# The order of a fused attention and FP4 feed-forward block: a table of places instead of a formula of due dates

## The chip, the cores and the metric

The kernel runs on one core of a Trainium2 chip. Its engines work side by side, each through its own queue of instructions in the order in which the program lists them: TensorE (PE, matmuls; PEld is its loading of weights), VectorE (DVE), ScalarE (ACT), GpSimd (POOL) and SyncE (SP, which here only issues transfers; ACT issues a few as well). The metric is the time of one execution on the device in microseconds (us), the median of several runs.

## What is computed

The input has 16 sequences of 512 rows of 256 numbers, in float32. The reference, cut to what matters:

```python
q, k = favor(x @ Wq + bq), favor(x @ Wk + bk)  # 16 heads of 16 numbers
# favor(a): exp(a - max) over a head's 16 numbers, divided by (their sum + 1e-6)
v = x @ Wv + bv
context = ((q @ k.T) / (q.sum(-1) + 1e-6)) @ v  # no softmax: linear in k.T @ v
x = layernorm(x + context @ Wo + bo)
# fp4(a): in blocks of 16, scale = max|a| / 6, each number rounded to the FP4 grid, times scale
gate, up = fp4(x) @ fp4(w_gate).T, fp4(x) @ fp4(w_up).T  # 704 wide
h = silu(gate) * up
x = layernorm(x + fp4(h) @ fp4(w_down).T)
```

## The kernel before, in words

A tile has 128 rows; a sequence (a batch `b`) has four tiles, worked on as two pairs, so there are 32 pairs `i`. Each stage is a function that hands its operations to a `Plan`:

- `project` (per pair): TensorE turns x (L636), ScalarE copies it to SBUF (`transposed`, L639, tile xT), four groups of two matmuls give q and k of a tile (L778), VectorE adds the bias (L781) and takes each head's maximum (L786), GpSimd subtracts it (L790).
- `features` (per batch): ScalarE's exp (L801), VectorE's sums and reciprocals (L803 to L814), GpSimd's scaling (L820).
- `key_values` (per batch): a sum over k on VectorE (L829, ks), k times x on TensorE (L836), copied by ScalarE (L843), times the weights of v (L852, L853), masked by VectorE (L857, kvT), times Wo (L864), copied by ScalarE (L870, M).
- `attend` (per pair): q turned (L636, copied at L639 as qT), times M (L892), then `norm`: sum with the input on VectorE (L733), mean and variance on ScalarE (L740, L742), the root on GpSimd (L746 to L748), applied on ScalarE (L755). The result goes to DRAM (L903) and is read back later (L910).
- `weight_scales` and `fp4_exact`: the three weights of the feed-forward part are quantised once, on VectorE, ScalarE and GpSimd (L515 to L534 and L563 to L584), in 12 pieces, and turned by TensorE (L597, L620).
- `quantise` (per pair): `codes` finds scales and FP4 codes of x on VectorE and ScalarE (L655 to L668); VectorE transposes them in blocks (L921, L691); four kinds of transfers through DRAM regroup the codes (L676, L681) and spread the scales over the partitions (L699, L704); GpSimd multiplies both (L929, xqT).
- `gate_up` (per pair): 16 matmul operations of 352 columns (L957; the chip runs each as two matmuls), silu on ScalarE (L962), product on VectorE (L964), `codes` of h, transposes (L1002), the same kinds of transfers, and GpSimd's product (L1009, hq, in four quarters). The last pair takes a shorter way, by L977 on VectorE and transposes on TensorE (L991).
- `down` (per pair): 12 matmul operations for each of its two tiles u (L1026), `norm`, and the output (L1038). The last two pairs have another norm (L718 to L725).

What sets the order is the plan. Every operation has an engine, a cost in us that the source estimates (`t_pe`, `t_dve`, `t_act`, `t_ts`, `t_pool` and figures beside the operations) and a **due date**, a multiple of `PAIR` = 25 that a formula gives from batch, pair and stage (`due_at`, `wdue`). `Plan.order` runs a list schedule of these estimates while the kernel is built: for each engine it finds the operations whose inputs are planned, and the earliest start of each, from its inputs' ends plus `LAG` where they are on another engine, the engine's own free time, free buffers and PSUM banks, and a port that `port=True` operations of VectorE share with GpSimd. Among those that can start within 0.02 us of the earliest on that engine it takes the one with the lowest due date:

```python
first = min(t for t, _ in c)
t, o = min(((t, o) for t, o in c if t <= first + 0.02), key=lambda x: (x[1].due, x[1].at))
if best is None or t < best[0]:
    best = t, o
```

The sequence that results is written out as the program. On the chip each engine follows its part of it and waits for data where it must; the planned times are not used there. `dma` makes two operations of a transfer: its issue on a queue (SP or ACT) and its flight.

Of the kernel before, what the change touches and what calls it, by code (L numbers as in the profile page):

```python
# [17 lines left out]
P = 128  # L18
# [8 lines left out]

LAG = 0.3

PAIR = 25.0  # L30
# [13 lines left out]
MAGIC_U = 1.5 * 2.0**29  # L44
UNTIE = 1.0 + 2.0**-17


# [44 lines left out]
class Op:  # L92
    __slots__ = ("eng", "us", "fn", "due", "preds", "succs", "left", "bufs", "new", "start", "end", "table", "port", "name", "at")


class Plan:
# [47 lines left out]
    def order(self):  # L144
# [32 lines left out]
        def start(o, at):  # L177
            if o.port:
                at = max(at, port)
            for p in o.preds:  # L180
                at = max(at, p.end + (LAG if p.eng != o.eng else 0.0))
            taken = {}
            shared = [b for b in o.new if isinstance(b, Bank) and id(b) not in ends]
            if shared:
                found = find(shared[0].args[0], [b.tag for b in shared])
                if found is None:
                    return None
                at = max(at, found[0])
            for b in o.new:
                if id(b) in ends or isinstance(b, Bank):  # L190
                    continue
                key = id(b.args[0]), b.tag
                ring, n = rings.setdefault(key, []), taken.get(key, 0)
                taken[key] = n + 1
                if len(ring) + n >= b.bufs:
                    left, end = ends[id(ring[n - b.bufs])]
                    if left:
                        return None
                    at = max(at, end + LAG)
            return at  # L200

        while len(out) < len(self.ops):
# [16 lines left out]
            o.start, o.end = t, t + us  # L219
            free[o.eng] = o.end  # L220
            if o.port:
# [11 lines left out]
            for b in o.bufs:  # L233
                left, end = ends.get(id(b), (b.users, 0.0))
                ends[id(b)] = left - 1, max(end, o.end)
            for s in o.succs:
# [9 lines left out]
def t_pe(n):  # L246
    return 2 * (n / 1200.0 + 0.002)


def t_dve(n):  # L250
    return 0.15 + n / 960.0


def t_act(n):
    return 0.16 + n / 1200.0

# [5 lines left out]
def t_pool(n):  # L262
    return 0.07 + n / 525.0


@with_exitstack
def tile_favor_fp4_block(
# [229 lines left out]
    def weight_scales(src, src_b, n, at, name, due):  # L497
# [37 lines left out]

        op("DVE", 11 * fast + 0.0063 * nb, due, rest, ins=[pb], outs=[sc_b, *iv])
        return part, sc_b, iv

    def fp4_exact(src, src_b, scales, sc_b, iv, k, name, due):
# [7 lines left out]
        def b3(ap):  # L547
# [5 lines left out]
        pw, px = (psum("pg", f"{t}_{name}{k}") for t in ("pw", "px"))  # L553
        d, g, a = t_dve(F2), t_pool(F2), t_act(F2)
        tt, gt, act = nc.vector.tensor_tensor, nc.gpsimd.tensor_tensor, nc.scalar.activation
# [25 lines left out]
        op("ACT", a, due, lambda: act(y(), upper(m()), AF.Identity, bias=magic[:, 2:3], scale=UNTIE), ins=[M], outs=[px])  # L581
        op("DVE", t_ts(F2), due, lambda: nc.vector.tensor_scalar(c(), lower(y()), 6, None, ALU.logical_shift_left),
           ins=[px], outs=[pr])
# [58 lines left out]
    def codes(src, xn, sq, dst, key, n, scales, at, name, due, sat=None):  # L642
# [18 lines left out]

        op("DVE", 0.27 + 0.0073 * nb, due, scale, ins=[(amax, key)], outs=[(nscale, key), (inv, key)])
        op("DVE", t_dve(n), due, lambda: nc.vector.scalar_tensor_tensor(  # L663
# [8 lines left out]
    def regroup(src, dst, n, tag, name, due):  # L672


        d = Buf(dr, [P, 4, n], "g" + tag, 3, f"g_{name}", U32)
        dma(f"g{name}", 3.0, due, lambda: nc.sync.dma_start(d.tile, src.tile), ins=[src], outs=[d])  # L676

        def back():
            rows = d.tile.rearrange("(a i) q n -> i a q n", i=32)
            for q in range(4):  # L680
                nc.sync.dma_start(dst[32 * q : 32 * q + 32, :, :], rows[:, :, q, :])  # L681

        dma(f"h{name}", 3.5, due, back, ins=[d], outs=[dst], issue=1.8)

    def spread_scales(nscale, G, dst, tag, name, due, holds=()):
# [7 lines left out]
            nscale.tile.rearrange("p (u g r) -> p g r u", u=2, r=n),  # L693
        ), ins=[nscale], outs=[sT], port=True)
        d = Buf(dr, [2 * n, G, P], "d" + tag, 3, f"d_{name}")

        def write():
            for a in range(0, P, 32):
                nc.sync.dma_start(d[:, :, a : a + 32], sT[a : a + 32, :, :])  # L699

        dma(f"w{name}", 4.0, due, write, ins=[sT], outs=[d], issue=1.8)
        into, dst_b = dst

        dma(f"r{name}", 3.0 + 0.7 * G, due, lambda: nc.sync.dma_start(  # L704
            into(), d.tile.rearrange("(r u) g t -> r (u g t)", u=2).unsqueeze(1).to_broadcast([n, 8, 2 * G * P])),
            ins=[d], outs=[dst_b], holds=holds)

    def norm(pr, add, dst, name, due, ins, r, junk, us=range(2)):
# [3 lines left out]
        if n == 1:  # L712
# [9 lines left out]

            op("DVE", 2 * t_dve(D) + 0.1, due, stats, ins=[(pr, key)] + ins, outs=[(r, key), st, mv])
            op("POOL", 0.7, due, lambda: nc.gpsimd.tensor_tensor(rstd.tile, mv[:, 1:2], neg_half[:, :1], ALU.pow), ins=[mv], outs=[rstd])
            op("DVE", t_dve(D), due, lambda: nc.vector.tensor_scalar(  # L725
# [10 lines left out]

        op("DVE", n * (t_dve(D) + 0.06), due, total, ins=[(pr, key)] + ins, outs=[(r, key), rs])

# [10 lines left out]

        op("ACT", 0.35 + 0.6 * n, due, square, ins=[(r, key), rs], outs=[(dst, key), var, nm])  # L750
        op("POOL", 1.1, due, root, ins=[nm], outs=[var, rstd, nb])

# [5 lines left out]

        op("ACT", 0.6 * n, due, apply, ins=[(r, key), nb, rstd], outs=[(dst, key)])

# [33 lines left out]
    def features(b, due):  # L794
# [20 lines left out]

        op("DVE", 1.2, due, recip, outs=[s, r], port=True)
        for t in range(TPB):
# [6 lines left out]
    def key_values(b, due):  # L824
# [3 lines left out]
        ks = buf([D], "ks", 2, f"ks_{b}")  # L828
        op("DVE", t_dve(TPB * D), due, lambda: nc.vector.tensor_reduce(  # L829
            ks.tile, qk[:, :, D:].rearrange("p t d -> p d t"), AX.X, ALU.add), ins=[qk], outs=[ks])  # L830
# [24 lines left out]
        kvT = buf([DC, P], "kvT", 2, f"kvT_{b}")  # L855
        op("PE", DC * (DC + 1) * t_pe(P), due, mm_kv, ins=[xk, ks, wqkv_in], outs=[pkv], holds=[kvT], name="kv")
        op("DVE", t_dve(DC * P), due, lambda: nc.vector.tensor_tensor(  # L857
# [18 lines left out]
    def attend(b, p, due):  # L876
# [7 lines left out]
        xb = buf([2, D], "xb", 2, f"xb_{i}")  # L884
        op("POOL", 1.4, due, lambda: nc.gpsimd.tensor_tensor(xb.tile, x[:, two, :], twice(b_o), ALU.add),  # L885
           ins=[x, wo_in], outs=[xb])
# [15 lines left out]
        d = Buf(dr, [P, 2, D], "x1", NP, f"dx1_{i}")  # L902
        dma(f"wx1_{i}", 3.0, due, lambda: nc.scalar.dma_start(d.tile, x1.tile), ins=[x1], outs=[d], queue="ACT")  # L903
        st[i] = {"d": d}


    def quantise(i, due):
        x1 = st[i]["x1"] = buf([2, D], "x1", X1, f"x1_{i}")
        d = st[i]["d"]
        dma(f"rx1_{i}", 3.5, due - PAIR, lambda: nc.sync.dma_start(x1.tile, d.tile), ins=[d], outs=[x1])  # L910
        n = 2 * D
# [10 lines left out]
            xw.tile.rearrange("p q (u t) -> p q u t", u=2),  # L922
            xc.tile.bitcast(U32).rearrange("p (u q t) -> p q u t", u=2, q=4)), ins=[xc], outs=[xw], port=True)
        regroup(xw, xcT, 2 * 32, "x", f"x{i}", due)
# [3 lines left out]
        for u in range(2):  # L928
            op("POOL", t_pool(D), due, lambda u=u: nc.gpsimd.tensor_tensor(  # L929
                xqT[:, DC * u : DC * (u + 1), :].rearrange("p c (a t) -> p c a t", t=32),  # L930
# [6 lines left out]
    def gate_up(i, due):  # L937
# [32 lines left out]
        if i >= NP - LAST:  # L970
            for u in range(2):
# [9 lines left out]

                op("DVE", t_dve(FF), d, dequantise, ins=[(hc, u), (scales[1], u)], outs=[hd], port=True)
                for j, (gs, n) in enumerate(((range(TG - 1), P), (range(TG - 1, TG), LW))):
# [3 lines left out]
                    def tr(gs=gs, n=n, pt=pt, hd=hd):  # L987
# [6 lines left out]
                    eng, copy = (("ACT", nc.scalar.copy), ("DVE", nc.vector.tensor_copy))[j]  # L994
                    op(eng, t_act(k * P), d, lambda u=u, gs=gs, n=n, k=k, pt=pt, copy=copy: copy(
                        hq()[:n, u, gs[0] : gs[-1] + 1, :, :].rearrange("p g c t -> p (g c) t"), pt[:n, :k, :]),
# [4 lines left out]
        for u in range(2):  # L1001
            op("DVE", 0.15 + TG * P / 960.0, d, lambda u=u: nc.vector.transpose(  # L1002
                hw.tile.rearrange("p q (u g t) -> p u q g t", u=2, g=TG)[:, u], words()[:, u]),
               ins=[(hc, u)], outs=[(hw, u)], port=True)
        regroup(hw, hcT, 2 * TG * 32, "h", f"h{i}", d)
        spread_scales(scales[1], TG, (lambda: flat()[:, NQ : NQ + 2 * TG * P], (both, "s")), "h", f"h{i}", d)
        for u in range(2):
            for c in range(2):
                op("POOL", t_pool(TG * P), d, lambda u=u, c=c: nc.gpsimd.tensor_tensor(  # L1009
                    hq()[:, u, :, c, :].rearrange("p g (a t) -> p g a t", t=32),  # L1010
# [4 lines left out]
    def down(i, due):  # L1015
# [6 lines left out]
        for u in range(2):  # L1022
            for f in range(2 * TG):
# [4 lines left out]
                    start=f == 0, stop=f == 2 * TG - 1,  # L1028
                ), ins=[(both, f"{u}{c}{int(g == TG - 1)}"), wdT_b], outs=[(pd, u)], holds=[r], name="down")
        y = buf([2, D], "y" if i < NP - 1 else "yl", 1, f"y_{i}")  # L1030
        out2 = out[b, 2 * p * P : 2 * (p + 1) * P, :].rearrange("(u p) d -> p u d", p=P)

        for us in ((0,), (1,)) if i >= NP - 2 else (range(2),):
# [4 lines left out]
            dma(f"y{i}_{us[0]}", 2.5, due, lambda t=t, eng=eng: eng.dma_start(out2[:, t, :], y[:, t, :]),  # L1038
                ins=[(y, None if len(us) == 2 else us[0])], queue=q)

# [24 lines left out]
    for i in range(NP):  # L1065
        quantise(i, (i - 1.2) * PAIR)
        gate_up(i, i * PAIR)
        down(i, (i + 3) * PAIR)

    with tc.manual_schedule():  # L1070
# [47 lines left out]
```

## Time and profile before

| | us |
|---|---|
| runs | 792.51, 789.62, 791.81 |
| their median | 791.81 |
| the profiled execution, first to last instruction (span) | 792.0 |
| TensorE busy in it | 768.6 (97%) |
| VectorE busy | 656.7 (83%) |
| GpSimd busy | 455.9 (58%) |
| ScalarE busy | 416.5 (53%) |
| mean granted clock of TensorE | 0.995 |
| transfers | 89.23 MB, mean 113 GB/s |

The times are device times of whole runs; the profile is of one more execution, whose span is 0.2 us over the median. A row of the profile names the source line, the engine, the operation and what it writes and reads, then how often it ran, how long it was busy and the mean of one in ns; behind a second bar stands the idle time of the engine just before such instructions and what ended it. A row of busy times by stage gives the stretch, its length, then the busy time of each engine with the number of its instructions, the granted clock of TensorE, the share of the transfer engines in use, and GB/s.

### The profile page before, as it was taken

The page shows a single profiled execution, that of the slowest core. Times are in us where ns is not written, and L with a number is a line of the kernel's source. Part 1 is how long each engine was busy: PE and PEld are TensorE (multiplying, and loading weights), DVE is VectorE, ACT ScalarE, POOL GpSimd, SP SyncE. Part 2 cuts the span into 40 slices and gives each one's busy share as a digit, 9 for nine tenths or more (in the row PEclk, how much of TensorE's full clock was granted, in tenths as well). Part 3 has the DMA queues.
Part 4 walks back from the last instruction along what each step waited for, and adds up shares of the span by engine and source line. Part 5 has one row for each costly group of instructions (what it writes and reads, how often), then busy time and mean ns, then how long its engine had stood idle before and what let it go on. Part 6 is the DMA issues. An engine that isn't in the chain of part 4 may idle for free.

```text
span 792.0 us, 10915 instructions
## 1 busy us (share of the span) xinstructions
PE 768.6 (97%) x3118; PEld 552.5 (70%) x3118; DVE 656.7 (83%) x1340; ACT 416.5 (53%) x893; POOL 455.9 (58%) x602
## 2 busy tenths in 40 slices
PE   7999999989998999999999999999999999999996
PEld 3567657657676777767777777777777777777774
DVE  2998999999888798697697798888878988778784
ACT  2347766868887783544545444444334444344441
POOL 5668788889887755574554435434533543543633
PEclk9999999999999999999999999999999999999998
DMA  9112411211111044404335454554554554464441
GB/s 277 45 55 86 142 53 54 82 60 62 54 53 62 30 129 133 118 37 124 100 112 138 145 171 136 152 149 134 149 154 135 145 149 140 125 179 129 136 130 41
DMA packets 104348, 89.23 MB, mean 113 GB/s; under 512 B 44512, under 2 KB 87904, under 8 KB 104288
## 3 DMA queue, kind: packets, MB, share of 16 engines
q1 hardware_dynamic: 90704, 71.49, 31.8%
q10 hardware_dynamic: 13584, 17.04, 6.0%
q8 instruction: 25, 0.41, 0.2%
q14 instruction: 35, 0.29, 0.1%
HBM read 53.28 MB, written 35.21 MB: 112 GB/s over the span
## 4 chain that ended last, share of the span: by engine, by line
PE 62%; DVE 12%; DMA 8%; POOL 8%; issue 4%; ACT 4%; SPq 2%; ACTq 0%; POOLq 0%; DVEq 0%
PE bank L957 26%; PE bank L1026 14%; PE bank L778 8%; PE bank L892 5%; PE bank L836 5%; POOL hq L1009 3%; DMA out_dram<-y 3%; DVE qk L781 2%; PE bank L636 2%; DVE mx L786 2%; DMA hcT<-g_h 2%; SPq L681 1%; POOL xqT L929 1%; DVE fs L803 1%; PE bank L852 1%
## 5 line engine op out<-in xcount | busy, mean ns | idle before, releaser
L957 PE MATMUL bank<-w_guT,xqT 128*128 128x352 f32 x1024 | 311.3, 459 | 0.0
L957 PEld LDWEIGHTS bank<-w_guT,xqT 128*128 128x128 f32 x1024 | 193.8, 190 | 100.4 <-ACT g L962 0.2
L1009 POOL TENSOR_TENSOR hq<-hcT,hq 128x384 f32<-128x384 bf16 x124 | 127.3, 1058 | 179.3 <-DMA hcT<-g_h 101.4
L1026 PE MATMUL bank<-w_dT,hq 128*128 128x256 f32 (+1 forms) x768 | 173.1, 379 | 1.1 <-DVE r L718 1.1
L1026 PEld LDWEIGHTS bank<-w_dT,hq 128*128 128x128 f32 (+1 forms) x768 | 144.9, 190 | 27.5 <-issue 1.9
L778 PE MATMUL bank<-w_qkv,xT 128*128 128x512 f32 x256 | 120.8, 602 | 3.8 <-DVE qk L781 1.9
L964 DVE TENSOR_TENSOR h<-bank,g 128x352 f32<-128x352 f32 x128 | 65.7, 515 | 50.9 <-ACT g L962 24.1
L962 ACT ACTIVATE g<-bank 128x352 f32<-128x352 f32 x128 | 57.6, 458 | 87.7 <-PE bank L957 77.8
L666 ACT ACTIVATE sq<-h,magic 128x704 f32<-128x704 uint16 x64 | 56.2, 878 | 79.2 <-DVE h L663 78.6
L820 POOL TENSOR_TENSOR qk<-qk,fr 128x512 f32<-128x512 f32 x64 | 67.0, 1073 | 20.5 <-DVE fr L814 18.9
L790 POOL TENSOR_TENSOR qk<-qk,mx 128x512 f32<-128x512 f32 x64 | 67.4, 1068 | 19.2 <-DVE mx L786 19.0
L778 PEld LDWEIGHTS bank<-w_qkv,xT 128*128 128x128 f32 x256 | 46.6, 193 | 45.4 <-issue 35.8
L755 ACT ACTIVATE y<-r,nb_d,rstd_d 128x256 f32<-128x256 f32 x60 | 32.6, 591 | 59.2 <-POOL nb_d L748 59.2
L929 POOL TENSOR_TENSOR xqT<-xcT,xs 128x256 f32<-128x256 bf16 x64 | 46.3, 740 | 27.6 <-DMA d_h<-sT_h 23.4
L836 PE MATMUL bank<-qk,x 128*128 128x256 f32 x256 | 59.7, 387 | 2.1 <-ACT qT L639 2.1
L892 PE MATMUL bank<-M,qT 128*128 128x256 f32 x256 | 59.6, 381 | 1.8 <-ACT M L870 1.8
L655 DVE TENSOR_REDUCE bank<-h 128x44 f32<-128x704 f32 x64 | 57.1, 893 | 1.6
L663 DVE SCALAR_TENSOR_TENSOR h<-h,bank 128x704 f32<-128x704 f32 x64 | 56.7, 886 | 2.1
L836 PEld LDWEIGHTS bank<-qk,x 128*128 128x128 f32 x256 | 49.5, 195 | 12.7 <-ACT qT L639 3.4
L781 DVE TENSOR_TENSOR qk<-bank,b_qkv 128x512 f32<-128x512 f32 x64 | 43.0, 681 | 18.3 <-PE bank L778 17.9
L892 PEld LDWEIGHTS bank<-M,qT 128*128 128x128 f32 x256 | 47.8, 190 | 13.2 <-ACT M L870 3.8
L885 POOL TENSOR_TENSOR xb<-x,b_o 128x512 f32<-128x512 f32 x32 | 41.0, 1285 | 22.8 <-DVE r L733 22.7
(137 smaller groups left out, 1083.3 us busy)
## 6 DMA issues: line engine op xcount, KB each, us to landing
g_h<-hw SPq DMA_DIRECT2D x31, 384.0 KB, 2.8
hcT<-g_h SPq DMA_DIRECT2D x124, 96.0 KB, 2.4
hq<-d_h SPq DMA_DIRECT2D x31, 384.0 KB, 4.1
dx<-x1n ACTq DMA_DIRECT2D x32, 256.0 KB, 2.0
x<-dx SPq DMA_DIRECT2D x32, 256.0 KB, 3.1
x<-_attn_hidden_states_dram SPq DMA_DIRECT2D x15, 512.0 KB, 3.5
out_dram<-y ACTq DMA_DIRECT2D x30, 256.0 KB, 3.3
xs<-d_x SPq DMA_DIRECT2D x32, 128.0 KB, 2.5
```

The costliest lines, as they stand in the source:

```text
L655: op("DVE", t_dve(n), due, lambda: nc.vector.tensor_reduce(amax[:, g], b3(src()), AX.X, ALU.max, apply_absolute_value=True), ins=[src_b], ...
L778: op("PE", t_pe(D2), due, lambda c=c, u=u, pqk=pqk: nc.tensor.matmul(pqk.tile, xT[:, 2 * c + u, :], w_qkv[:, c, :D2], start=c == 0, stop=c ...
L781: op("DVE", t_dve(D2), due, lambda t=t, pqk=pqk: nc.vector.tensor_tensor(qk[:, t, :], pqk.tile, b_qkv[:, :D2], ALU.add), ins=[pqk], outs=[ ...
L790: op("POOL", t_pool(D2), due, lambda g=g: nc.gpsimd.tensor_tensor(qk3()[:, g, :], qk3()[:, g, :], bcast(mx[:, g], HD), ALU.subtract), ins= ...
L820: nc.gpsimd.tensor_tensor(f3, f3, bcast(r[:, t * 2 * H : (t + 1) * 2 * H], HD), ALU.mult)
L836: nc.tensor.matmul(pxk[:, c * D : (c + 1) * D], x[:, t, c * P : (c + 1) * P], qk[:, t, D:], start=t == 0, stop=t == TPB - 1,)
L892: nc.tensor.matmul(pu(pa.tile)[:, u, :], qT[:, 2 * u + c, :], M[:, c, :], start=c == 0, stop=c == DC - 1,)
L957: op("PE", t_pe(F2), due + u * 0.2 * PAIR, lambda c=c, u=u, lo=lo, ps_=ps_: nc.tensor.matmul(ps_[:, :F2], xqT[:, 2 * u + c, :], w_guT[:, c ...
L962: op("ACT", t_act(F2), due, lambda g=g, pg=pg: nc.scalar.activation(g.tile, pg[:, :F2], AF.Silu), ins=[pg], outs=[g], table="silu")
L964: op("DVE", t_dve(F2), due, lambda g=g, h=h, pu_=pu_, k=k: nc.vector.tensor_tensor(h[:, k * F2 : (k + 1) * F2], pu_[:, :F2], g.tile, ALU.m ...
L1009: op("POOL", t_pool(TG * P), d, lambda u=u, c=c: nc.gpsimd.tensor_tensor(hq()[:, u, :, c, :].rearrange("p g (a t) -> p g a t", t=32), hcT. ...
L1026: op("PE", t_pe(D), due, lambda f=f, g=g, c=c, n=n, u=u: nc.tensor.matmul(pu(pd.tile)[:, u, :], hq()[:n, u, g, c, :], w_dT[:n, f, :], star ...
```

## The change

No operation is added or taken away. Three things change in the plan, all of them used only while the kernel is built.

First, the due dates are replaced. A string holds two digits of base 91 for each of the 3939 operations in the order in which the source makes them; the number, from 0 to 1915, takes the place of `o.due`, just ahead of `order`. The table was found by a search. Some operations share a number.

Second, the estimates and lags are taken from a trace: `LAG` falls from 0.3 to 0.04; a matmul's result is there 0.165 us after its end for all but TensorE itself; a flight's end counts with 0.09 us in place of the lag; an engine is free again a little ahead of an operation's end (`OVER`). Lags now hold between operations of one engine too, but for TensorE. Many costs get new figures.

Third, three block transposes of VectorE (L691, L921, L1002) no longer share GpSimd's port in the plan, and the matmuls of `down` for tile 1 come after those for tile 0.

```diff
-LAG = 0.3
+LAG = 0.04
+DRAIN = 0.165
+OVER = {"DVE": 0.083, "ACT": 0.095, "POOL": 0.041}
+LANDED = 0.09
...
+DIGITS = "#$%&'()*+,-./0123456789:;<=>?@ABCDEFGHIJKLMNOPQRSTUVWXYZ[]^_`abcdefghijklmnopqrstuvwxyz{|}~"
+PLACES = (
+    "#3)<#5+B###%#B#$&k#2#?&B#@#9$.$1'<'C#<(v#=#:$i#>#;$}$4'R'M'l#,#(#'#&#-#.'r#c(k($')&U&}#7'('%'9+s)+&i'6(#(:#*'x'$'h&l'@'k"
...
-                at = max(at, p.end + (LAG if p.eng != o.eng else 0.0))
+                at = max(at, p.end if p.eng == o.eng == "PE" else p.done + LAG)
...
-            free[o.eng] = o.end
+            o.done = o.end + (DRAIN if o.eng == "PE" else LANDED - LAG if o.eng.startswith("DMA") else 0.0)
+            free[o.eng] = o.end - OVER.get(o.eng, 0.0)
...
-                ends[id(b)] = left - 1, max(end, o.end)
+                ends[id(b)] = left - 1, max(end, o.done)
...
 def t_pe(n):
-    return 2 * (n / 1200.0 + 0.002)
+    return 2 * (n / 1200.0 + 0.0027)
 def t_dve(n):
-    return 0.15 + n / 960.0
+    return 0.155 + n / 960.0
 def t_act(n):
-    return 0.16 + n / 1200.0
+    return 0.165 + n / 1200.0
 def t_pool(n):
-    return 0.07 + n / 525.0
+    return 0.075 + n / 520.0
+def t_mix(n):
+    return 0.19 + n / 475.0
...
-        op("DVE", 11 * fast + 0.0063 * nb, due, rest, ins=[pb], outs=[sc_b, *iv])
+        op("DVE", 2.0 + 0.015 * nb, due, rest, ins=[pb], outs=[sc_b, *iv])
...
-        dma(f"g{name}", 3.0, due, lambda: nc.sync.dma_start(d.tile, src.tile), ins=[src], outs=[d])
+        dma(f"g{name}", 2.4, due, lambda: nc.sync.dma_start(d.tile, src.tile), ins=[src], outs=[d])
...
-        dma(f"h{name}", 3.5, due, back, ins=[d], outs=[dst], issue=1.8)
+        dma(f"h{name}", 2.0, due, back, ins=[d], outs=[dst], issue=1.85)
...
-        ), ins=[nscale], outs=[sT], port=True)
+        ), ins=[nscale], outs=[sT])
...
-        dma(f"w{name}", 4.0, due, write, ins=[sT], outs=[d], issue=1.8)
+        dma(f"w{name}", 1.6, due, write, ins=[sT], outs=[d], issue=1.7 + 0.25 * G)
...
-        dma(f"r{name}", 3.0 + 0.7 * G, due, lambda: nc.sync.dma_start(
+        dma(f"r{name}", 1.3 + 0.75 * G, due, lambda: nc.sync.dma_start(
...
-        op("DVE", t_dve(TPB * D), due, lambda: nc.vector.tensor_reduce(
+        op("DVE", 1.95, due, lambda: nc.vector.tensor_reduce(
             ks.tile, qk[:, :, D:].rearrange("p t d -> p d t"), AX.X, ALU.add), ins=[qk], outs=[ks])
...
-        dma(f"rx1_{i}", 3.5, due - PAIR, lambda: nc.sync.dma_start(x1.tile, d.tile), ins=[d], outs=[x1])
+        dma(f"rx1_{i}", 2.7, due - PAIR, lambda: nc.sync.dma_start(x1.tile, d.tile), ins=[d], outs=[x1])
...
-                op("POOL", t_pool(TG * P), d, lambda u=u, c=c: nc.gpsimd.tensor_tensor(
+                op("POOL", t_mix(TG * P), d, lambda u=u, c=c: nc.gpsimd.tensor_tensor(
...
-                ), ins=[(both, f"{u}{c}{int(g == TG - 1)}"), wdT_b], outs=[(pd, u)], holds=[r], name="down")
+                ), ins=[(both, f"{u}{c}{int(g == TG - 1)}"), wdT_b] + [(pd, 0)] * u, outs=[(pd, u)], holds=[r], name="down")
...
+    assert len(PLACES) == 2 * len(plan.ops)
+    for o in plan.ops:
+        hi, lo = PLACES[2 * o.at : 2 * o.at + 2]
+        o.due = DIGITS.index(hi) * len(DIGITS) + DIGITS.index(lo)
```

L691 is shown with its `port=True` gone; L921 and L1002 lose theirs in the same way.

## The prediction

> **What bounds the kernel now.** I read the page first, then the busy times by stage, then the chain that ended last, then the instructions in order of time around the holes. The page says that TensorE is nearly full:
>
> ```profile
> span 792.0 us, 10915 instructions
> ...
> PE 768.6 (97%) x3118; PEld 552.5 (70%) x3118; DVE 656.7 (83%) x1340; ACT 416.5 (53%) x893; POOL 455.9 (58%) x602
> ```
>
> A busy PE need not be at its peak, so I take its real pace from runs of back-to-back matmuls in the chain (start, length, line, count):
>
> ```profile
> 214.43 6.01 PE bank L778 x14
> ...
> 249.49 0.44 PE bank L636 x4
> ...
> 253.84 3.45 PE bank L836 x16
> ...
> 259.88 0.45 PE bank L852 x4
> ...
> 473.11 5.18 PE bank L1026 x24
> 478.29 9.47 PE bank L957 x32
> ```
>
> Length over count gives 0.429 us (512 columns), 0.110 and 0.1125 (128), 0.2156 and 0.2158 (256) and 0.296 (352). With the counts of the groups, L957 takes 1024 x 0.296 = 303.1, L1026 768 x 0.2158 = 165.7, L778 256 x 0.4293 = 109.9, L836 and L892 256 x 0.2156 = 55.2 each, L864 64 x 0.2156 = 13.8, L636 256 x 0.110 = 28.2, L852 128 x 0.1125 = 14.4, L853 64 x 0.11 = 7.0, and the 46 transposes of L597, L620 and L991 about 5.3. The sum is **757.8 us**: the work of TensorE, which no order changes. The span holds 34.2 us more. 4.3 of it lie before the first matmul (4.26 in the timeline), 5.4 after the last one (it starts at 786.4). The other 24.5 are spacing over that pace, added up from the starts of neighbouring matmuls in the trace: 3.5 in 0 to 20, **17.3 in 20 to 260, under 0.2 in 260 to 760**, 3.7 after. The stages show the same (PE, PEld, DVE, ACT, POOL busy):
>
> ```profile
> 0.00:20.00 20.00, 15.09 (x41) 7.78 (x42) 6.11 (x7) 4.22 (x6) 10.58 (x22) 1.00 0.93 277
> 20.00:260.00 240.00, 229.40 (x1008) 161.59 (x1007) 220.91 (x394) 166.10 (x352) 193.78 (x239) 0.99 0.20 66
> 260.00:300.00 40.00, 40.00 (x166) 28.15 (x166) 33.44 (x71) 29.31 (x63) 25.70 (x35) 1.00 0.32 95
> 300.00:760.00 460.00, 460.00 (x1805) 336.60 (x1804) 377.30 (x830) 208.19 (x455) 213.62 (x292) 1.00 0.47 134
> 760.00:792.00 32.00, 24.14 (x105) 18.34 (x103) 18.90 (x42) 8.65 (x21) 12.22 (x17) 0.94 0.23 71
> ```
>
> So the kernel is bound by TensorE, but the loss is all in the first third and the last 30 us. VectorE is 92% busy in 20 to 260 and 82% in 300 to 760.
>
> The Trainium skill (Perfetto Trace Analysis, Identifying the Most-Contended Engine) would judge TensorE's headroom by its weight-load share, not its busy time. By that, 460 − 336.6 = 123 us would be free in 300 to 760, and the gain could be ten times what follows; the spacing there shows none, and the measurement decides.
>
> **What the holes are.** The largest, at 241.4, with the ACT rows ahead of it and the PE rows on both sides:
>
> ```profile
> 240.12 1.88 PE L778 MATMUL bank<-w_qkv,xT 128*128 128x512 f32 x4
> ...
> 241.02 0.49 ACT L742 ACTIVATE x1n<-r,nm_a 128x256 f32<-128x256 f32 x1
> ...
> 241.51 1.07 ACT L755 ACTIVATE x1n<-r,nb_a,rstd_a 128x256 f32<-128x256 f32 x2
> ...
> 243.44 0.59 ACT L639 COPY qT<-bank 128x512 f32<-128x512 f32 x1
> ...
> 244.08 5.41 PE L836 MATMUL bank<-qk,x 128*128 128x256 f32 x16 [2.08 <-ACT qT L639]
> ```
>
> The transposes for qT were done by 240.3, but their copy to SBUF stood on ScalarE behind two norms that nobody was waiting for. The cost is 2.2 us of idle, and then 1.7 more: the sixteen matmuls of L836 take 5.41 us here and 3.45 us at 253.84, and the granted clock is 0.57 in 245 to 249. The others have the same make: kvT (L857) waits on VectorE behind twelve instructions of one weight-scale operation (L515 to L534, 37.0 to 42.3), 1.3 us; M (L870) 0.6, 1.3 and 0.4; xT (L639) 0.5, 0.5, 0.5, 0.4 and 0.8; L781 0.5, 0.9, 0.9 and 0.5; a weight tile (L580) 1.2; L820 0.7. In each, something on VectorE, ScalarE or GpSimd that TensorE needs next stands behind something it needs later. An order can mend that.
>
> **The change part by part.** It adds and removes no instruction and no transfer, so each cost below is that of a moved place.
>
> *Estimates of the plan.* They run before the kernel is built; on the chip they cost nothing. What they alter is what the plan believes. The old plan charges L829 0.15 + 1024/960 = 1.22 us, where its row has 1.949 (x16): 11.7 us of VectorE, all in batches' chains, that it did not see. It charges L1009 0.07 + 384/525 = 0.80, where the row has 1.058 (x124): 32 us of GpSimd. The new figures are 1.95 and 1.00. For transfers it was too long: 5.1 + 0.45 us for hq<-d_h, where the median from issue to landing is 4.1; the new figure is 3.55 + 0.45. One figure stays too short: the weight scales at 37.0 take 5.3 us, old plan 4.8, new 4.6; once, 0.7 us at most.
>
> *Lag, drain, overlap, the port.* The lag between engines falls from 0.3 to 0.04 us, with 0.165 more behind a matmul. Three transposes (L691, L921, L1002) may stand beside GpSimd's work. Rows: 574 ns for L1002 where 0.15 + 384/960 gives 550; so 62 x 0.024 = 1.5 us of VectorE at most, hidden in the 82.7 us that it idles in 300 to 760.
>
> *u = 1 of down after u = 0.* TensorE runs 24 down matmuls of a pair in a row already; 0 to 0.9 us at the end, where two matmuls waited for L718.
>
> *Places.* A place decides only between operations of one engine whose earliest starts lie within 0.02 us, so the table is no timetable; data and buffers come first. All queues are reordered, SP's and ACT's DMA queues too.
>
> **The sum.** Before 10 us nothing moves: TensorE waits for loads and runs at half pace (L778 every 0.85 us), 3.1 us. The four holes from 15.7 to 42 (0.46, 0.46, 0.70, 1.26: 2.9) fall where only the first batches are loaded; I take a third, 1.0. The rest of 20 to 260 is 17.3 − 2.4 = 14.9 us. Between nothing and all of it I take four fifths, 11.9, by VectorE's row: it has 240 − 220.9 = 19.1 us idle in this stage, so with 12.9 taken out it still has 6, and what does not fit has 82.7 us later. At the end 3.7 us: half of it is the last pair's own chain (h, codes, L977, transposes), so a third, 1.2. In 260 to 760 nothing can be gained. Together 14.1: 792.0 − 14.1 = **778 us**. All 21.5 us of movable holes would give 770.5. The median of the runs shown, 791.81, is 0.2 under the span, so I leave the figure.
>
> The skill's clock rule (TensorE: Matmul & The Clock Gate, Part 1) sets half clock after an idle window of about 3.4 us. Here 2.1 us of idle was followed by it. By the rule the 1.7 us would not count with this hole, and the sum would be 779; I go by the row.
>
> **Rivals.** *The supply becomes the bound.* With no holes the steady part starts earlier, but its inputs need not. In pair 10 the last quarter of hq was written at 480.7 and L1026 began at 487.6; in pair 27 it is
>
> ```profile
> 734.56 3.87 POOL L1009 TENSOR_TENSOR hq<-hcT,hq 128x384 f32<-128x384 bf16 x4 [9.98 <-PE bank L957]
> ```
>
> written at 738.4, while L1026 begins at 736.71 and needs the last quarter only near its end. The cushion shrank by 8.6 us over 17 pairs; by its last matmul 3.2 are left. If the new order moves TensorE and not this chain, only those 3.2 us and some of the end come back: 787. For it: that shrinking. Against it: VectorE idles 18% of that stage, and mostly because it waits for matmuls or silu (L964).
>
> *Slower: late landings hold TensorE in the steady part.* The old plan leaves hw to hcT 3.45 + 1.8 + 3.5 = 8.75 us, the new one 2.85 + 1.85 + 2.0 = 6.7. Its figures are medians: landings of L681 go from 1.6 over 2.3 to 5.0, of L676 from 1.7 to 4.9, and in 480 to 740 g_h<-hw has 3.4, 0.6 over the page's 2.8. SP issues in the plan's order (a load at L394 stood there for up to 22.3 us until PE L836 freed its buffer), so a late landing holds what is queued behind it: the next pair's loads too. If the order puts hq just ahead of L1026 and each of 31 pairs loses 0.6 us, that is 18.6 us, against 14 won: 797. It decides from 0.45 us a pair. Against it: a late pair moves all later work, and gives the next transfer that time.
>
> *It does not do what it says.* If readiness decides nearly every choice, the order hardly changes: 791.
>
> **How the numbers follow.** Forecast 0.70 (772 to 784, at 778); supply 0.15 (784 to 790, four fifths of it under 787.8); no change 0.07; slower 0.08 at 796 to 800. A measurement of this kernel tells about 0.5% (4 us) from no change. Faster: 0.70 + 0.12 = 0.82; same 0.03 + 0.07 = 0.10; slower 0.08. The range 771 to 790 leaves out the slower case and most of "no change".
>
> **What would show it.** Right: PE busy at least 234 of 240 in 20 to 260 (or the same work ending some 12 us sooner); no PE wait for qT, M or kvT over 1 us; granted clock 1.00 at 240; VectorE over 95% busy there; L957 and L1026 in steady runs of 9.47 and 5.18 us, and the last matmul near 773. Wrong: waits of L1026 on L1009 or of L957 on L929 between 300 and 760, or new holes of 1 us in the first third behind an operation that the plan sizes too short.

## The result, and the profile after

The changed kernel is slower: **810.36 us** (median of 5 runs, 809.39 to 812.30) against 791.44 for the kernel before on the same chip (5 runs), a ratio of 1.0248 [1.0229, 1.0267]. The forecast was 778, the range 771 to 790; it is wrong in its sign. The profiled execution took 810.25 us, its span is 808.5.

Changed kernel, the page (busy times) and the busy times by stage, in the columns used before (PE, PEld, DVE, ACT, POOL, granted clock, transfers):

```profile
span 808.5 us, 10809 instructions
...
PE 773.5 (96%) x3118; PEld 551.9 (68%) x3118; DVE 640.1 (79%) x1340; ACT 414.8 (51%) x893; POOL 455.4 (56%) x602
```

```profile
0.00:20.00 20.00, 14.95 (x42) 7.72 (x43) 5.11 (x6) 3.53 (x5) 9.95 (x21) 1.00 0.93 274
20.00:260.00 240.00, 229.36 (x1001) 160.91 (x1000) 214.56 (x386) 160.29 (x343) 190.54 (x235) 0.99 0.20 67
260.00:300.00 40.00, 40.00 (x177) 29.04 (x176) 32.22 (x66) 30.45 (x65) 27.62 (x37) 1.00 0.19 62
300.00:760.00 460.00, 447.07 (x1725) 321.77 (x1724) 358.20 (x812) 205.67 (x448) 205.09 (x282) 1.00 0.46 133
760.00:808.00 48.00, 42.16 (x180) 32.42 (x178) 30.04 (x74) 14.85 (x34) 22.24 (x30) 0.99 0.30 86
```

Two rows carry the result. In 20 to 260 TensorE is busy 229.36 us, where it had 229.40: nothing was won. In 300 to 760 it had all 460 and now has 447.07: 12.9 us are lost where there had been none. Spacing over TensorE's pace, added up as in the prediction, says the same: 3.0 us in 0 to 20 (3.5 before), 17.3 in 20 to 260 (17.3), 19.7 in 420 to 800 (before, under 0.2 in 260 to 760 and 3.7 after). Set side by side, 260 to 760 lost some 18.5 us, and the start and the end won about 2, which leaves the 16.5 us by which the span grew.

The waits of TensorE, longest first (what waited, what ended it, us in total, times, longest), name what was late:

```profile
PE bank L1040 <- POOL xqT L1012: 10.6, 6, 3.1
PE bank L719 <- POOL mask L569: 4.5, 1, 4.5
PE bank L1109 <- POOL hq L1092: 2.4, 5, 1.4
PE bank L861 <- ACT xT L722: 2.3, 3, 1.2
PE bank L861 <- DVE wdn L617: 2.2, 1, 2.2
PE bank L719 <- DVE qk L864: 1.9, 1, 1.9
```

(L1040, L1109, L1012 and L1092 are the L957, L1026, L929 and L1009 of the prediction; each line stands 83 further down.) The first and third row are the steady part. One such hole in order of time, from GpSimd's, SP's and TensorE's rows:

```profile
431.00 1.41 POOL L1012 TENSOR_TENSOR xqT<-xcT,xs 128x256 f32<-128x256 bf16 x2 [8.29 <-DMA xs<-d_x]
```

```profile
424.74 1.92 SPq L782 DMA_DIRECT2D d_x<-sT_x  x4
426.84 0.54 SPq L787 DMA_DIRECT2D hq<-d_h  x1
427.42 0.60 SPq L787 DMA_DIRECT2D xs<-d_x  x1
```

```profile
429.58 0.39 PE L936 MATMUL bank<-ks,b_qkv 128*128 128x128 f32 x2
431.77 2.63 PE L1040 MATMUL bank<-w_guT,xqT 128*128 128x352 f32 x8 [1.80 <-POOL xqT L1012]
```

GpSimd had idled for 8.29 us when the scales xs landed, 3.6 us after their issue (their median in 400 to 780 is 2.6), and TensorE was through with all that its queue held ahead of these matmuls. SP had issued the four writes of d_x and the read for hq just before, 0.4 to 0.5 us each. In the whole of 300 to 760 GpSimd's product for xqT waited for xs like this (us, times), first in the changed kernel, then in the one before (us, times, longest):

```profile
  DMA xs<-d_x: 59.9, 11
```

```profile
POOL xqT L929 <- DMA xs<-d_x: 2.3, 2, 1.5
```

GpSimd writes a pair's xqT in two halves, one for each tile. From the end of such a write to the first matmul that reads it, taking the shorter of the two, pairs 12 to 30 had 11.8 us falling to 2.8 in the kernel before; now six of the nineteen have 0.2 us or less.

The start has another story. VectorE's rows:

```profile
20.51 3.10 DVE L592 TENSOR_REDUCE bank<-wgu 128x176 f32<-128x2816 f32 x1 [3.74 <-DMA wgu<-in_L_ffn_w_up_dram]
23.52 1.28 DVE L864 TENSOR_TENSOR qk<-bank,b_qkv 128x512 f32<-128x512 f32 x2
24.71 0.34 DVE L607 TENSOR_SCALAR bank<-bank 128x176 f32<-128x176 f32 x1
```

The table sends the loads of x2 and x3 ahead of the weights' (SP began those at 6.62; before, at 4.89), while the plan takes the weights as landed at a fixed 16.0 us. The last part that L592 needs landed at 18.9 before and at 20.5 now. VectorE stood 3.74 us for it (1.88 before) with finished sums of L864 queued behind, then did the scale operation from 24.7 to 30.0 (5.3 us, planned 4.64), and TensorE had four holes of 0.7 to 2.4 us by 40, the first of them until that scale operation was done (the row of L861 and wdn above). So 20 to 40 lost 7.7 us of spacing (1.3 before), and 40 to 260 lost 9.5 (16.0 before): **6.4 us were won and lost again**.

### The profile page after: what moved, and what is told of

Same layout as the page of the kernel before. It is cut to its first block, busy times and chain, and to the rows that moved or that the text cites. A ratio compares the mean times of both kernels' runs of the same rounds, so it can differ in the third digit from the quotient of the medians.

```text
span 808.5 us, 10809 instructions
## 1 busy us (share of the span) xinstructions
PE 773.5 (96%) x3118; PEld 551.9 (68%) x3118; DVE 640.1 (79%) x1340; ACT 414.8 (51%) x893; POOL 455.4 (56%) x602
## 4 chain that ended last, share of the span: by engine, by line
PE 58%; DVE 15%; DMA 11%; POOL 5%; SPq 4%; issue 4%; ACT 3%; ACTq 0%; POOLq 0%; DVEq 0%
PE bank L1040 21%; PE bank L1109 12%; PE bank L861 8%; PE bank L919 6%; PE bank L975 5%; DVE bank L738 2%; DMA x<-dx 2%; POOL hq L1092 2%; PE bank L719 2%; SPq L764 2%; DMA hcT<-g_h 2%; PE bank L947 1%; DVE fs L886 1%; PE bank L935 1%; DMA xs<-d_x 1%
## 5 line engine op out<-in xcount | busy, mean ns | idle before, releaser
L1040 PE MATMUL bank<-w_guT,xqT 128*128 128x352 f32 x1024 | 329.6, 461 | 10.6 <-POOL xqT L1012 10.6
L1040 PEld LDWEIGHTS bank<-w_guT,xqT 128*128 128x128 f32 x1024 | 193.9, 191 | 100.9 <-POOL xqT L1012 13.8
L1109 PE MATMUL bank<-w_dT,hq 128*128 128x256 f32 (+1 forms) x768 | 189.1, 380 | 3.6 <-POOL hq L1092 2.4
L1092 POOL TENSOR_TENSOR hq<-hcT,hq 128x384 f32<-128x384 bf16 x124 | 123.0, 1022 | 111.8 <-DMA hcT<-g_h 95.7
L1109 PEld LDWEIGHTS bank<-w_dT,hq 128*128 128x128 f32 (+1 forms) x768 | 144.1, 190 | 47.0 <-POOL hq L1092 7.9
L861 PE MATMUL bank<-w_qkv,xT 128*128 128x512 f32 x256 | 121.3, 600 | 4.8 <-ACT xT L722 2.3
L1012 POOL TENSOR_TENSOR xqT<-xcT,xs 128x256 f32<-128x256 bf16 x64 | 48.1, 772 | 74.1 <-DMA xs<-d_x 59.9
L861 PEld LDWEIGHTS bank<-w_qkv,xT 128*128 128x128 f32 x256 | 46.6, 192 | 43.1 <-issue 33.3
L864 DVE TENSOR_TENSOR qk<-bank,b_qkv 128x512 f32<-128x512 f32 x64 | 43.4, 684 | 26.2 <-PE bank L861 25.9
L751 DVE TENSOR_SCALAR hcs<-sq 128x704 uint16<-128x704 uint16 x64 | 38.8, 608 | 16.2 <-ACT sq L749 15.9
```

What stands on the lines that cost most here:

```text
L861: op("PE", t_pe(D2), due, lambda c=c, u=u, pqk=pqk: nc.tensor.matmul(pqk.tile, xT[:, 2 * c + u, :], w_qkv[:, c, :D2], start=c == 0, stop=c ...
L1040: op("PE", t_pe(F2), due + u * 0.2 * PAIR, lambda c=c, u=u, lo=lo, ps_=ps_: nc.tensor.matmul(ps_[:, :F2], xqT[:, 2 * u + c, :], w_guT[:, c ...
L1092: op("POOL", t_mix(TG * P), d, lambda u=u, c=c: nc.gpsimd.tensor_tensor(hq()[:, u, :, c, :].rearrange("p g (a t) -> p g a t", t=32), hcT.t ...
L1109: op("PE", t_pe(D), due, lambda f=f, g=g, c=c, n=n, u=u: nc.tensor.matmul(pu(pd.tile)[:, u, :], hq()[:n, u, g, c, :], w_dT[:n, f, :], star ...
```

## Experiments

The theory from these rows: the new order leaves the steady part no spare time, so that lateness on SP's queue, from landings or issues, goes through to TensorE. Its rivals: SP is simply too busy for any order that fills the start; or the late start carries on to the end; or, later, the new estimates are at fault and not the table. Every run has its own runs of the kernel before beside it.

### 1. Does SP's time or one landing set the steady part?

*after_free*: the regrouping read (hcT, xcT) reads a constant buffer and so waits for no landing; the real codes are left out.

```diff
+        for t, n in (("x", 2 * 32), ("h", 2 * TG * 32)):
+            consts[t] = dr.tile([P, 4, n], U32, tag="c" + t, name="c" + t, bufs=1)
...
-            rows = d.tile.rearrange("(a i) q n -> i a q n", i=32)
+            rows = consts[tag].rearrange("(a i) q n -> i a q n", i=32)
```

> The changed order with one link cut: the four transfers that bring the codes back (hcT and xcT, L764 in the changed kernel) read a buffer of zeros that is written once, so they no longer wait for the codes' way out to land. Number of issues, bytes and order of every engine stay. It leaves out the codes, so the feed-forward part is computed from zeros. Theory A (the table leaves no cushion, and what is late on the transfer path goes into TensorE from 430 us on): the 19 us of holes between 400 and 800 us go, 810.4 becomes 790 to 794. Rival B (the table's order of VectorE, GpSimd and TensorE is itself poor, the transfers are only the last link): most holes stay, 803 to 810.

812.73 us, 1.0249 [1.0214, 1.0283]: nothing gained, TensorE busy 447.06 in 300 to 760. The landing of g is not the cause by itself. The run left the scales' way as it was, and GpSimd's product for xqT still waited 53.1 us for xs (10 times); no run here took that link away.

*after_extra* and, later, *before_extra*: from pair 12 on SP issues one more transfer of 2 KB behind the read-back of x1.

```diff
...
+            if i >= 12:
+                t = dr.tile([P, 4], F32, tag=f"extra{i}", name=f"extra{i}", bufs=1)
+                nc.sync.dma_start(t, magic)
...
```

> The changed order; behind each of the 20 read-backs of x1 from pair 12 on stands one more small transfer on SP (0.5 us of issue, nobody waits for it). Theory A with SP's issue time on the path: up to 20 x 0.55 = 11 us more, 816 to 821. Theory A with late landings alone, or rival B: 810 to 812.

> The kernel before, with the same 20 extra small transfers on SP. Theory A: its cushion (11.8 us at pair 12, 2.8 left at pair 30) is used up late: 0 to 12 us over before, less than the 20 us that they cost the changed kernel. Rival B (SP's time is the limit in any order): 15 to 20 us over before.

832.09 us for after_extra, 1.0496 [1.0457, 1.0535], some 20 us over the changed kernel for 20 issues of 0.43 us: each costs over twice its own length, more than any theory had expected. Some 5 us of it are matmuls at half pace behind three of the longer holes, where the granted clock was 0.57 to 0.61 over 4 us. before_extra has 798.27 against 793.39, 1.0086 [1.0052, 1.0121], 4.9 us for the same by the medians and 6.8 by the ratio, against 8.6 us of issues. So lateness on SP reaches the end more than in full in the new order, and in part in the old one.

*after_rx*: 20 of the read-backs issued by ScalarE.

```diff
+        back_on = nc.scalar if i >= 12 else nc.sync
-        ... lambda: nc.sync.dma_start(x1.tile, d.tile) ...
+        ... lambda: back_on.dma_start(x1.tile, d.tile) ...
```

> The changed order; from pair 12 on the read-back of x1 (x<-dx, 0.54 us of issue each plus a gap of about 0.1) is issued by ScalarE at the same place of the plan, not by SP: 20 issues fewer on SP. Theory A with SP's issue time as the late term: up to 20 x 0.6 = 12 us less, 798 to 804. Theory A with late landings alone: 807 to 811. Rival B: no change, 810.

815.54 us, 1.0265 [1.0216, 1.0314]: relieving SP of 20 issues (ScalarE then carries them) gains nothing, so its busy time as such is not the bound. These issues take 0.38 us in the median, not 0.54, so about 10 us and not 12 were at stake. The Trainium skill (DMA: Bandwidth & Descriptors, Issuing engines are not separate DMA queues) says that spreading transfers over issuers saves only the time to start them, usually small beside the transfer. Moving 20 agrees with it. What an added issue costs the work queued behind it is another matter, and was 1 us here.

*after_start*: weights requested ahead of x2 and x3, and the weight maximum and the scale operation put behind sums that were ready.

> The changed order but for the first 40 us: the feed-forward weights are requested before the rows of batches 2 and 3, and on VectorE the two operations that wait for them (L592, and L598 to L617 behind it) stand behind two sums and two reductions that were ready. Theory A: the plan took the weights to be there at 16.0 us, they came at 20.4; the 6.5 us that the chip was behind the plan at 50 us shrink by 2 to 5, and that is kept to the end: 805 to 808. Rival C (a late start is absorbed by later waits): 810.

813.18 us, 1.0257 [1.0221, 1.0293]. No gain at the end, but hardly any at the start either. VectorE no longer stood for the weights before L592, and spacing in 20 to 40 was 7.8 us for 7.7: TensorE now waited longer for the end of the scale operation.

```profile
PE bank L861 <- DVE wdn L617: 3.2, 1, 3.2
```

So the late weights do not explain the start's loss by themselves; where that operation stands seems to do more of it. Whether a mended start would be kept to the end is not shown by this run.

### 2. Is it that the table plans no cushion?

*table_300*: operations that the plan starts before 300 us keep their places, the rest goes by the old formula. *table_300_start* adds the moves of after_start, *table_300_extra* the 20 transfers.

```diff
+    by_table = {k for lo, hi in BY_TABLE for k in range(lo, hi)}
...
-        o.due = DIGITS.index(hi) * len(DIGITS) + DIGITS.index(lo)
+        o.due = DIGITS.index(hi) * len(DIGITS) + DIGITS.index(lo) if o.at in by_table else 10000.0 + o.due
```

> Order half undone: operations that the plan of the changed kernel starts before 300 us keep their places of the table, all later ones go back to the formula of due dates (behind the table's), with the new estimates kept. By the program's own plan the end stays at 779.6 us, as for the changed kernel, but the rescaled codes xqT now stand ready 12 to 27 us before TensorE reads them, where the table plans 0.3 to 5 us for most pairs. Theory A (the table left no cushion, so every late issue and landing of the steady part reaches TensorE): the waits for xqT and hq after 400 us go, 787 to 793 us. Rival B (SP and the transfers are too slow in the steady part whatever the order): 803 to 812.

> As table_300, and the three moves of after_start on top (weights requested ahead of the loads of x2 and x3; the weight maximum and the scale chain behind ready sums). In after_start itself nothing of this was seen at the end. Theory A: the start's 1 to 2 us are now kept, since the steady part no longer absorbs them by its own waits: 1 to 3 us less than table_300, 785 to 791. Rival B: as table_300 within 1 us, 803 to 812.

> As table_300, with one more small transfer issued by SP in each of the 20 pairs from pair 12 on, as in after_extra, where the same 20 issues cost 20 us. Theory A: with 12 us and more of cushion they cost 0 to 3 us over table_300. Rival B (SP's time itself is the limit): 15 to 20 us over table_300.

821.52 us, 1.0356 [1.034, 1.0372]; 822.49, 1.0366 [1.0349, 1.0383]; 837.25, 1.0533 [1.0493, 1.0573]. **The theory of the cushion fell.** xqT was ready 5 to 10 us ahead of its reader in pairs 12 to 30 (12 to 27 in the plan), and the kernel was slower still: slower than either theory had expected, and the 20 extra transfers cost 15.7 us on top, where theory A had 0 to 3 and rival B 15 to 20. TensorE now waits for banks that VectorE frees late, and SP's longest wait is one that no data explains. table_300, TensorE's waits in 300 to 760 and SP's in 400 to 780:

```profile
PE bank L1043 <- DVE r L819: 10.0, 9, 2.4
```

```profile
SPq L767 <- DMA out_dram<-y: 54.5, 19, 4.9
```

L767 reads codes; it has nothing to do with the output y. The compiled program shows why it waits: landings are counted on eight counters in turn, over SP's and ScalarE's transfers alike, and a transfer waits until the one eight places before it has landed. An output write that ScalarE issues late thus holds SP, and all that is queued on it. In the kernel before the same wait is as large, and TensorE loses nothing there:

```profile
SPq L681 <- DMA out_dram<-y: 56.3, 18, 5.0
```

*after_noy* and *table_300_noy* leave out the output writes of pairs 10 to 29.

> The changed kernel without the output writes of pairs 10 to 29 (they are left out, so 20 of 32 pairs' results are not stored; the norm ahead of them stays). In the program a transfer waits until the one eight places before it has landed, whatever it carries, so SP waits for output writes that ScalarE issues late: 22.6 us of SP's waits in 400 to 780 have this end. Theory L (these borrowed waits are a large part of the steady loss): 796 to 805. Rival (the replay: they hide beside other waits): 807 to 811, at most 3 us less than the changed kernel.

> table_300 (821.5 us) without the same 20 output writes. There SP's waits that end with an output write are 54.5 us in 400 to 780. Theory L: 11 us and more less than table_300, 811 or below. Rival: 818 to 822.

808.16 us, 1.0197 [1.0153, 1.024], and 809.98, 1.0225 [1.0189, 1.026]. Without the 20 writes table_300 is 11.5 us faster, and the changed kernel 2 (4 by the ratios, whose intervals overlap). The runs also take 20 transfers away, so this is the most that the borrowed waits can be charged with: clear in table_300, and not the changed kernel's main loss.

### 3. Is it the table, or the estimates that came with it?

*formula_new* is the changed kernel without its table. *formula_pad* is that with the transfers' old, longer flights; *formula_lag* is formula_new with the old LAG; *before_flight* is the kernel before with only the new flights.

```diff
-    assert len(PLACES) == 2 * len(plan.ops)
-    for o in plan.ops:
-        hi, lo = PLACES[2 * o.at : 2 * o.at + 2]
-        o.due = DIGITS.index(hi) * len(DIGITS) + DIGITS.index(lo)
```

> The changed kernel without its table: the formula of due dates, with all the new estimates. The program's own plan then ends at 805.6 us, all its holes of TensorE before 300 us, and gives xqT 12 us of cushion and more after that. Theory D (the new estimates of the transfers are the usual landing times, with nothing for late ones; an order made with them queues work on SP and POOL right behind each landing, so that a late one holds all that is queued after it, table or formula): holes appear after 300 us on top, 820 to 845 us. Rival T (the table alone is at fault, the estimates are good): about the plan, 803 to 810.

> As formula_new, with only the six estimates of the transfers' flight put back to the longer ones of the kernel before (g 3.0, h 3.5, w 4.0, r 3.0 + 0.7 G, the write and the read-back of x1 3.0 and 3.5 us); durations of the engines' operations and SP's issue stay new. The plan ends at 790.5 us. Theory D: 793 to 804, its steady part without waits for xqT or hq, and at least 20 us less than formula_new. Rival B (SP and the transfers are too slow in the steady part whatever the order): 805 and more, with the same growth after 300 us as formula_new. Rival T: about the plan, 790 to 795, and formula_new near its own plan too.

> The kernel before with one part of the change alone: the six shorter estimates of the transfers' flight, nothing else. The program's plan ends at 806.6 us with its holes before 300 us, and none after. Theory D: slower than that plan by what late landings cost after 300 us, 812 to 832 us. Rival T (table at fault): 803 to 809, near the plan, and no waits of TensorE for xqT, hq or banks after 300 us.

> formula_new (838.5 us) with only LAG put back from 0.04 to 0.3 us, its transfers' estimates left short. The plan ends at 798.8 us, its holes before 300 us. Theory D2 (any slack in the plan serves, the 0.3 us at every hand-over between engines as well as longer flights): 800 to 812, at most 8 us of growth after 300 us, against 22 in formula_new. Rival (only the estimates of the transfers matter): 815 and more.

| | us | ratio to before | TensorE busy, 20 to 260 | of 460 in 300 to 760 |
|---|---|---|---|---|
| formula_new | 838.50 | 1.0555 [1.0515, 1.0594] | 216.03 | 445.07 |
| formula_pad | 807.34 | 1.0169 [1.0133, 1.0204] | 224.42 | 455.37 |
| formula_lag | 825.06 | 1.0399 [1.0364, 1.0434] | 228.91 | 442.32 |
| before_flight | 809.42 | 1.0177 [1.0133, 1.0222] | 221.57 | 460.00 |

The table is not to blame alone: with the new estimates the formula is slower than the table by 28 us (24 by the ratios). Longer flights in the plan win 31 us, 10 of them in the steady part (more than half of its loss); a longer LAG wins 13, none of them there. formula_new came out as theory D had it, formula_pad 3 us over its range. But before_flight has short flights and loses nothing after 300 us: 809.42 is near its plan's 806.6, as rival T had it, and formula_lag went the rival's way as well. So "short estimates of flights cost the steady part" holds beside the new estimates of the engines' operations and not beside the old ones; which of the old figures keeps that order safe was not found.

### 4. An order that bears late landings

If lateness is what the order must bear, a search that knows of it should win. Three orders were searched in a replay of the program and written out whole:

```diff
...
+        seq = sorted(plan.ops, key=lambda o: o.due)
+        banks = dict.fromkeys(b for o in seq for b in o.new if isinstance(b, Bank))
+        for b, k in zip(banks, BANKS):
+            b.place = int(k)
-        for o in plan.order():
+        for o in seq:
```

> Same operations and buffers as the changed kernel, another order, written out whole (a place for each operation and a bank for each PSUM tile, so that the plan's estimates no longer matter). It was found by moving one or two operations at a time in a replay of the program: every engine in its order, with the changed kernel's durations, SP's issue times as the traces have them (0.33 to 0.60 us an issue, 0.04 to 0.1 between), each transfer waiting for the landing of the eighth before it, and the weights landing 6.1 us after their request. A move is kept if the mean end over draws falls in which every flight is its median times a random factor (sigma 0.33 of its logarithm, about the spread of the traces). Theory D (the order of the change is good only if nothing lands late): 776 to 786 us, no steady growth of waits. Rival B (SP or transfers too slow in the steady part for any order that fills the start): 795 and more.

> The control of order_late: the same start, the same moves and the same replay, but with every flight at its median, one draw. The replay then ends at 777 us, 2.5 us sooner than order_late's does at the medians. Theory D: on the chip it is slower than order_late by 8 to 20 us (787 to 802), with waits for xqT, hq or banks after 300 us. Rival (late landings do not matter, only the wrong start and SP's issue times did): 775 to 783, at or below order_late.

> As order_late (789.58 us; its trace ran within 1 us of the replay up to 560 us, and then lost 3 us twice, once beside an issue of SP that took 1.48 us where its like take 0.42), searched further from there with two things harder: the flights' random factor wider (sigma 0.36), and 3 in 100 issues 1.0 us longer. The replay's mean end falls from 785 to 782 us. Theory D (what the order has to bear is lateness): 780 to 788, at or under order_late. Rival (the rest is not lateness): 788 to 792.

| | us | ratio to before | TensorE busy, 20 to 260 | of 460 in 300 to 760 |
|---|---|---|---|---|
| order_median | 794.52 | 1.0016 [0.9999, 1.0032] | 237.46 | 449.84 |
| order_late | 789.58 | 0.9956 [0.9938, 0.9975] | 236.86 | 455.13 |
| order_late2 | 782.17 | **0.9872 [0.9853, 0.9892]** | 237.05 | 460.00 |

All three fill the first third alike; they differ in the steady part, in the order in which they were made to bear lateness. At the medians the replay had put order_median first (777, order_late 2.5 later). order_late and order_median lie 4.9 us apart, where 8 to 20 were expected, and order_late missed its own range (776 to 786) by 3.6, so the size was missed twice. order_late2 came in inside its range. It was searched for longer than order_median, which has part in that difference; how much is not shown. order_late2 beats both kernels: 10.2 us under the one before, and its span is 780.0. With it the rival falls by which SP or the transfers are too slow in the steady part for any order that fills the start. Its stages and, after 300 us, order_median's waits of TensorE (of order_late2 there are none):

```profile
20.00:260.00 240.00, 237.05 (x1052) 168.53 (x1053) 221.63 (x396) 162.19 (x343) 194.04 (x237) 1.00 0.20 64
...
300.00:760.00 460.00, 460.00 (x1794) 336.23 (x1793) 376.18 (x845) 207.24 (x470) 217.49 (x301) 1.00 0.49 141
```

```profile
PE bank L1117 <- POOL hq L1100: 6.2, 5, 2.7
PE bank L1048 <- POOL xqT L1020: 3.9, 4, 2.1
```

L1117 and L1048 are L1109 and L1040 of the changed kernel: order_median waits for the same two things. The spare time at xqT goes the same way. Counted as above, 0.2 us or less is left in six of the pairs 12 to 30 of order_median, as in the changed kernel, in two of order_late and in one of order_late2.

## Why the prediction was wrong

- **TensorE's floor and the holes of before: right.** order_late2 has the forecast's marks: over 234 us busy in 20 to 260, all 460 in 300 to 760, and 6.7 us of spacing in 20 to 260 where 17.3 had been, so 10.6 regained by an order (forecast 11.9). One mark did not come: VectorE is 92% busy there (221.63 of 240 us), not 95, and has 18.4 us to spare, so the room on VectorE by which the prediction chose its four fifths did not set the gain.
- **"I take four fifths, 11.9": wrong for this table.** It won 6.4 us in 40 to 260 and lost 6.4 in 20 to 40. The prediction priced the too short scale operation at "0.7 us at most" and was right about that figure alone; it did not ask where the table puts this operation, nor see that the plan holds the weights' landing at a fixed 16.0 us. VectorE stood 3.74 us for them with ready work behind, and TensorE then 2.2 us for the scale operation. after_start took the first wait away and the second grew to 3.2, so the place of the scale operation seems to weigh more; how the 6.4 us divide is not shown. The mark was named ("new holes of 1 us in the first third"), the step was not worked out.
- **"In 260 to 760 nothing can be gained": true, and the step that failed.** The sum entered that stage as zero, although it could only lose, and left the one loss it knew of to a rival. The stage lost some 18.5 us, 13.0 of them in TensorE's waits for xqT and hq. With the start's gain missing as well, this is the way from 778 to the span of 808.5.
- **The slower rival: right in kind and place, wrong in its chance, and near in size partly by luck.** It named waits of L1040 on L1012 and of L1109 on L1092, and SP holding what is queued behind a late landing, and priced them at 18.6 us in the steady part, where some 18.5 were measured. But it took 0.6 us from each of 31 pairs; in the trace seven holes of 1.3 to 3.3 us hold 13 of it. Its total of 797 was short by 13, since it kept the 14 us won elsewhere. It was given 0.08, for "a late pair moves all later work, and gives the next transfer that time". The runs contradict that: in the new order SP's lateness is not given back, and 20 more issues cost 20 us. The prediction had itself read the spread of the landings (L681: 1.6, 2.3, 5.0) and the step from 8.75 to 6.7 us in the plan, and then did not charge them.
- **Its mechanism was finer than priced.** "SP holds" is part of it: after_free, after_rx and after_noy each took one piece away and gained nothing or, the last, 2 to 4 us. What is shown is that the order decides how much lateness TensorE sees (20 us against 4.9 to 6.8 for the same extra issues; the same operations in order_late2 wait for neither xqT nor hq after 300 us). That late landings and issues are what the changed order fails to bear rests on these and on order_late against order_median, 4.9 us; no run took the lateness itself out of the changed kernel. Shown as well is that cushion at xqT alone does not suffice (table_300). Which estimate of before made its order safe stays open.
- **"0.2 under the span, so I leave the figure": a slip of about 2 us.** In the runs made later a time is 1.7 to 2.0 us over the span of the same execution, so the span of 792.0 was that of an execution some 2 us slower than the median. It changes nothing in what failed.
- **Estimates "cost nothing on the chip": true as written, and misleading.** They decide the order as much as the table does: formula_new against formula_pad is 31 us without an instruction changed.
- **Supply rival (787) and no change (791)**: neither came; the order did change, and the steady part fell behind instead of keeping its pace. The shrinking cushion of hq was read from two pairs, 10 and 27 (6.9 and -1.7 us); in the same trace pair 9 has 2.6 and pair 28 has 3.9, so the fall is less steady than it seemed.

## What to carry to other kernels

A schedule made from measured durations is as good as what it knows of lateness: of three orders the one by medians ended first on paper and last on the chip. Of the two searched against a spread of landings, the first ended 3 to 5 us over its replay's mean of 785 (span and time), and the second, which was searched further and also against long issues, about at its 782. Where engines follow fixed queues, a stage without a hole is where a new order can only lose, so price that loss first: see how late the transfers land at worst, who is queued behind each, and what spare time is left. And check what a plan holds fixed (here the weights' landing, 2.9 us late in the kernel before and 4.5 now) before you trust it with a new order.

## What the runs showed of the hardware

- An extra transfer of 2 KB takes 0.43 us of SP and lands after 3.5 us (median; 2.5 to 5.8); it cost the changed kernel 1 us each, and the kernel before 0.25 to 0.34.
- Landings of one kind spread widely. In 300 to 780 of the changed kernel, from issue to landing, shortest, median and longest: L764 1.6, 2.4 and 5.3 us, L759 1.7, 2.6 and 5.2.
- The clock fell behind short idle again: 0.64 was granted in 40 to 44 us, after holes of 2.4, 2.1 and 1.7 us between 27 and 38, and 0.57 in 749 to 753, after 3.1 us of idle. Each cost some 1.5 us more, by the starts of the matmuls at half pace.
